# Heads of a latent-attention layer: output weights made in whole blocks, contexts ordered behind scores, query weights made at a border of the projection

## The chip, the cores and the metric

The kernel runs on one core of one Trainium2 chip. Time is device time in microseconds of one execution. Before the change three executions gave a median of 1743.06 us (1740.99 to 1744.13). One more execution was profiled.

## The reference, cut to what matters

Two layers over 4 sequences of 512 tokens and 1024 features. The part that the change touches is the attention of the second layer: 32 heads whose keys and values come from a latent of 64 numbers per token, shared by all heads.

```python
q = _rmsnorm(x @ wq_a.T, q_a_ln_w) @ wq_b.T            # 32 heads x (64 + 64 rotated)
kv = _rmsnorm(ckv, kv_a_ln_w) @ wkv_b.T                # from the latent, 64 wide
k_nope, v = (kv[..., :NOPE], kv[..., NOPE:])           # 64 and 128 per head
scores = jnp.einsum('bqhd,bkhd->bhqk', q_full, k_full) * softmax_scale
scores = jnp.where(causal[None, None], scores, jnp.finfo(scores.dtype).min)
attn = jax.nn.softmax(scores, axis=-1)
out = jnp.einsum('bhqk,bkhd->bqhd', attn, v).reshape(B, S, H * VD)
return out @ wo.T
```

Around it stand an attention over the batch, two feed-forward blocks with low-rank experts, layer norms and residual sums; the change leaves them alone.

## The kernel before

The kernel never forms keys or values per head. The key weights are multiplied into the query weights (`prepare_query`, L677), so that a query (`query`, L714) meets the latent itself; and the value weights are multiplied into the output weights (`prepare_output`, L1052), so that the attention's context stays 64 wide and two heads fill 128 rows.

Most products are in split precision: a float32 operand is kept as a high part in the fast format and a low part with the rest, and `matmul3` (L148) makes low x high, high x low, high x high (L150 to L152). "High" is a cast on ACT, "low" is a subtraction (operand minus high).

**Units.** The heads run as 128 units: 4 groups of 8 heads, in each the 4 sequences, in each the 8 heads. Unit u's steps are spread over the main loop (L1215): its query is made three units ahead and rotated (ACT copy L729, two DVE products into the one buffer `wA` L731 and L732, two POOL operations L733 and L734), split one unit ahead (DVE L741, POOL L742), its scores are made in four row tiles of 512, 384, 256 and 128 keys (`scores`, L898), each followed on DVE by mask and row minimum (L919) and on ACT by the exponential (L922); one unit later the probabilities are transposed on TensorE and copied out (`turn`, L934: two copies on ACT, one on DVE, L945). Three units later, for every second unit, `context` (L948) multiplies the probabilities of two heads with the latent: 16 float32 matmuls (L959) that each use 64 of the array's columns, two heads side by side, into one PSUM bank, and DVE divides by the sums (L962).

**Fillers.** Between these steps the loop advances a generator, `per` = three numbers of steps per unit (L1222), at three places: after the context, after the scores, after the next query. For a sequence after the first of a group the generator is the output projection of the sequence before it, `project` (L1008): for each pair of token tiles seven products of half matrices (names b11, t1, t2, b22, t3, b21, t4) in two steps of three matmuls each, into the PSUM banks `poa` and `pob` in turn, then DVE adds to the residual `xs` (L1036); ACT and POOL split the contexts (`cxh` L993, `cxl` L994), DVE forms their sums (`s`, L985). In the second half of a group's first sequence (in group 0: during all of it) the generator is `prepare_output`: it fills the 14 weight tiles of 128 x 512 (seven names, two of each) as high and low.

**How the output weights are made.** `block(n, half, at)` (L1063) multiplies one pair of heads' value weights with their output weights, 512 of 1024 columns at a time, into `poa` or `pob` (L1069, again 64 columns of the array and two side by side; the trace counts four matmuls per half). `kept` (L1077) copies a bank to one of six places in the buffer `raw` on ACT, `high` (L1080) casts on ACT, `low` (L1086) subtracts, `less` (L1094) takes differences. [...] After the second half of a pair `fetch_output` (L1043) loads the next pair into `slotC` by three DMAs; there is one such buffer. A block comes every two to four steps.

**Query weights.** `fetch_query` (L656) clears part of `raw` on POOL and issues six DMAs on SP; the main loop calls it twice in each group's last sequence, at units 0 and 4. `prepare_query` runs three units after the first (unit 3 of the last sequence) and four units after the second (unit 0 of the next group), in bank `pob`, between two fillers. `raw` has one buffer, for query weights and output weights in turn.

**What sets the order.** A planner orders the instructions of each engine at compile time: it walks through them by program order as priority and takes the first whose operands it expects to be ready by its own table of durations. Engines then run their list strictly in order, with semaphores. `tc.issue_after(ins)` adds an edge without a semaphore: what is traced inside it stands behind `ins` on that instruction's engine. All DMAs are issued on SP, also in order.

Of the kernel before, what the change touches and what calls it, by code (L numbers as in the profile page):

```python
# [46 lines left out]
def block_kernel(ctx: ExitStack, tc: tile.TileContext, a: dict, out: bass.AP):  # L47
# [100 lines left out]
    def matmul3(ps, ah, al, bh, bl, start, stop, **kw):  # L148

        T.matmul(ps, lhsT=al, rhs=bh, start=start, stop=False, **kw)  # L150
        T.matmul(ps, lhsT=ah, rhs=bl, start=False, stop=False, **kw)  # L151
        T.matmul(ps, lhsT=ah, rhs=bh, start=False, stop=stop, **kw)  # L152
# [693 lines left out]
    with ExitStack() as c2:  # L846
# [21 lines left out]
        scored = [None]  # L868
# [29 lines left out]
        def scores(u):  # L898
# [10 lines left out]
            for i in range(TPB - 1, -1, -1):  # L909
# [4 lines left out]
                else:  # L914
                    at = slice((i - 1) * P, i * P)
                    matmul3(ps[:, 0:n], h[:, at], l[:, at], kT[:, 0, 0:n], kT[:, 1, 0:n],
                            start=True, stop=True)
# [30 lines left out]
        def context(u):  # L948
# [7 lines left out]
            for j in range(TPB):  # L956
                w = S - j * P
                for n in range(2):
                    T.matmul(ps[n * KVR : (n + 1) * KVR, S - w : S], lhsT=k[:, j, :],  # L959
                             rhs=pTs[u + n][:, AT[j] : AT[j] + w], start=(j == 0),  # L960
                             stop=(j == TPB - 1))
# [46 lines left out]
        def project(g, b):  # L1008
# [7 lines left out]
            for j in range(0, TPB, 2):  # L1016
                at, xs, banks = {}, {}, {}
# [34 lines left out]
        def prepare_output(g, fetched):  # L1052
# [10 lines left out]
            def block(n, half, at):  # L1063
                nonlocal fetched
                wo, wv = fetched
                po[at] = pso.tile([P, 512], F32, name="po" + at)
                with ExitStack() if g else tc.issue_after(scored[0].ins):
                    for k in range(2):
                        T.matmul(po[at][k * KVR : (k + 1) * KVR, :], lhsT=wv[:, k, :],  # L1069
                                 rhs=wo[k][:, half * 512 : half * 512 + 512], start=True, stop=True)  # L1070
                if half and n + 1 < len(prs):
# [22 lines left out]
            def less(to, a0, a1):  # L1094
                if not {to, a0, a1} & set(po):
# [5 lines left out]
            def steps():  # L1101
                block(0, 0, "a")
                yield
                kept(0, "a")
                high("b11", "a")
                block(0, 1, "b")
                yield
                low("b11", "a")
                kept(1, "b")
                yield  # L1110
                less("b", "b", 0)
                block(1, 0, "a")
                yield
                high("t1", "b")
                kept(0, "b")
                kept(2, "a")
                high("b21", "a")
                yield
                low("t1", "b")
                low("b21", "a")  # L1120
# [610 lines left out]
```

## Time and profile before

| what | value |
|---|---|
| median of three executions | 1743.06 us |
| the profiled execution | 1745.28 us |
| its span, first to last instruction | 1743.1 us |
| TensorE busy (matmuls) | 1703.5 us, 98% |
| VectorE (DVE) busy | 1305.5 us, 75% |
| ScalarE (ACT) busy | 902.6 us, 52% |
| GpSimd (POOL) busy | 925.4 us, 53% |
| granted TensorE clock, mean | 0.998 |
| the heads, first to last unit | about 424 to 1490 us |
| from one context to the next in a steady stretch (802.56 to 818.66) | 16.1 us, two units |
| one block of output weights, half of the columns (L1069, four matmuls) | 1.08 us |
| one 128 x 512 subtraction on POOL (L1096) and on DVE (L1099), median | 1287 and 695 ns |

PE is TensorE, PEld its weight loads, SP the queue that issues DMAs. In a timeline a line gives start, duration, engine, line of the kernel, operation, written tile <- read tiles, shape, count, and in brackets the idle time before it with what ended it. In a line of waits stand the waiting group, what it waited for, the total, the number and the longest. In a window line stand the window, its length, and for PE, PEld, DVE, ACT and POOL the busy time with the number of instructions, then the clock, the DMA share and GB/s. Matmuls overlap in the pipeline, so the pitch from start to start is what counts, not a matmul's own duration; and a busy TensorE can still lose time between starts.

### The profile page before, as it was taken

The numbers are of one execution on the slowest core, as the hardware profiler recorded it, in microseconds if no ns is written. First come the engines' busy times: TensorE is split into PE (matmuls) and PEld (weight loads), VectorE is DVE, ScalarE is ACT, GpSimd is POOL, SyncE is SP. The second block draws the span as 40 slices with busy tenths as digits, with TensorE's granted clock in tenths as the row PEclk, the third lists the DMA queues.
The fourth block names the chain that finished last, engine by engine and source line by source line (L and its number), as shares of the span: only waits on it lengthen the run. The fifth ranks groups of instructions, "written<-read, shape, count | busy, mean of one in ns | idle before, by whom it ended". The sixth has DMA issues, their size and how long they took to land.

```text
span 1743.1 us, 31732 instructions
## 1 busy us (share of the span) xinstructions
PE 1703.5 (98%) x10536; PEld 1431.2 (82%) x10536; DVE 1305.5 (75%) x3494; ACT 902.6 (52%) x2316; POOL 925.4 (53%) x926
## 2 busy tenths in 40 slices
PE   7999999999999999999999999999999999999999
PEld 6899999998667877767787767777767777789998
DVE  7977885677877777787777777777778776687675
ACT  7422331366765555475555476555476555453332
POOL 0553541203666664666666656666566664575454
PEclk9999999999999999999999999999999999999999
DMA  4313543245324234353333353342454333853331
GB/s 195 134 40 118 181 164 114 89 139 164 115 87 150 81 109 150 104 176 114 110 122 113 105 201 97 105 140 95 133 168 151 103 111 120 303 196 122 138 117 62
DMA packets 131940, 228.17 MB, mean 131 GB/s; under 512 B 22272, under 2 KB 58752, under 8 KB 128448
## 3 DMA queue, kind: packets, MB, share of 16 engines
q1 hardware_dynamic: 131776, 226.13, 38.4%
q8 instruction: 84, 1.38, 0.3%
q14 instruction: 80, 0.66, 0.1%
HBM read 156.60 MB, written 71.83 MB: 131 GB/s over the span
## 4 chain that ended last, share of the span: by engine, by line
PE 85%; DVE 6%; DMA 3%; ACT 2%; issue 2%; POOL 2%; SPq 0%; ACTq 0%; DVEq 0%; POOLq 0%
PE psv L959 8%; PE pst L943 7%; PE po L150 4%; PE po L152 4%; PE po L151 4%; PE pss L150 4%; PE pss L151 4%; PE pss L152 3%; PE pob L150 3%; PE psq L150 3%; PE psq L151 3%; PE psq L152 3%; PE poa L150 3%; PE acc L150 3%; PE acc L152 3%; PE acc L151 3%
## 5 line engine op out<-in xcount | busy, mean ns | idle before, releaser
L922 ACT ACTIVATE p<-p,mn 128x512 f32<-128x512 f32 (+3 forms) x512 | 284.7, 558 | 218.0 <-DVE mn L919 217.6
L919 DVE CUSTOM_DVE_ANT_0 p<-pss,causal 128x512 f32<-128x512 f32 (+3 forms) x512 | 232.4, 486 | 27.4 <-PE pss L152 21.8
L733 POOL TENSOR_TENSOR qf<-qf,ropeT 64x512 f32<-64x512 f32 x128 | 164.6, 1286 | 166.4 <-ACT qf L729 163.4
L943 PE MATMUL pst<-ident,p 128*128 128x128 f32 x1280 | 186.4, 274 | 4.0 <-ACT pT L945 4.0
L734 POOL TENSOR_TENSOR qf<-qf,wA 64x512 f32<-64x512 f32 x128 | 164.4, 1285 | 29.9 <-DVE wA L732 23.4
L943 PEld LDWEIGHTS pst<-ident,p 128*128 128x128 f32 x1280 | 153.4, 141 | 31.4 <-ACT pT L945 8.7
L742 POOL TENSOR_TENSOR ql<-qf,qh 128x384 fp32r<-128x384 f32 x128 | 131.1, 1024 | 62.9 <-DVE qh L741 44.3
L994 POOL TENSOR_TENSOR cxl<-s,cxh 128x256 fp32r<-128x256 f32 x128 | 96.5, 762 | 120.6 <-ACT cxh L993 66.9
L945 ACT COPY pT<-pst 128x512 f32<-128x512 f32 x256 | 142.2, 577 | 23.2 <-PE pst L943 21.6
L150 PE MATMUL pss<-kT,ql 128*128 128x512 f32 (+2 forms) x384 | 142.8, 372 | 0.5 <-POOL ql L742 0.2
L150 PE MATMUL po<-w_h,hTl 128*128 128x384 f32 (+1 forms) x384 | 133.0, 346 | 0.5 <-DVE x L433 0.5
L151 PE MATMUL pss<-kT,qh 128*128 128x512 f32 (+2 forms) x384 | 130.9, 341 | 0.0
L152 PE MATMUL po<-w_h,hTh 128*128 128x384 f32 (+1 forms) x384 | 130.1, 339 | 0.0
L152 PE MATMUL pss<-kT,qh 128*128 128x512 f32 (+2 forms) x384 | 129.8, 338 | 0.0
L151 PE MATMUL po<-w_l,hTh 128*128 128x384 f32 (+1 forms) x384 | 129.7, 338 | 0.0
L945 DVE COPY pT<-pst 128x256 f32<-128x256 f32 x128 | 54.3, 424 | 94.2 <-PE pst L943 93.1
L729 ACT COPY qf<-psq 128x512 f32<-128x512 f32 x126 | 73.8, 586 | 71.9 <-PE psq L152 71.8
L731 DVE TENSOR_TENSOR wA<-psq,ropeT 32x512 f32<-32x512 f32 x126 | 87.7, 696 | 22.4 <-ACT qf L729 19.5
L994 POOL TENSOR_TENSOR cxl<-cx,cxh 128x256 fp32r<-128x256 f32 x96 | 73.5, 767 | 56.1 <-ACT cxh L993 53.5
L922 ACT ACTIVATION_READ_ACCUMULATOR p<-p,mn 128x1 f32 x512 | 97.0, 189 | 0.0
L150 PEld LDWEIGHTS pss<-kT,ql 128*128 128x128 f32 x384 | 72.1, 188 | 20.9 <-issue 3.6
L732 DVE TENSOR_TENSOR wA<-psq,ropeT 32x512 f32<-32x512 f32 x126 | 87.1, 691 | 1.7
(511 smaller groups left out, 4976.9 us busy)
## 6 DMA issues: line engine op xcount, KB each, us to landing
xs<-x_d SPq DMA_DIRECT2D x128, 256.0 KB
x_d<-xs SPq DMA_DIRECT2D x128, 256.0 KB
slotC<-in_woT_dram SPq DMA_DIRECT2D x32, 512.0 KB
rb<-r_d SPq DMA_DIRECT2D x128, 128.0 KB
w_t<-raw SPq DMA_DIRECT2D x32, 288.0 KB
x<-in_x_dram SPq DMA_DIRECT2D x16, 512.0 KB
x_d<-x SPq DMA_DIRECT2D x32, 256.0 KB
slotA<-q_d SPq DMA_DIRECT2D x8, 1024.0 KB
```

Source lines behind the costliest of these rows:

```text
L150: T.matmul(ps, lhsT=al, rhs=bh, start=start, stop=False, **kw)
L151: T.matmul(ps, lhsT=ah, rhs=bl, start=False, stop=False, **kw)
L152: T.matmul(ps, lhsT=ah, rhs=bh, start=False, stop=stop, **kw)
L733: G.tensor_tensor(f[mid], f[mid], ropeT[mid, 0, :], ALU.mult)
L734: G.tensor_tensor(f[mid], f[mid], t2[mid], ALU.add)
L742: G.tensor_tensor(l, f[:, P:S], f32(h), ALU.subtract)
L919: turn_of[0] = V.tensor_tensor_reduce(out=to, in0=ps[:, 0:n], in1=causal[:, S - n : S], scale=1.0, scalar=-NEG, op0=ALU.add, op1=ALU.min, ...
L922: A.activation(to, to, AF.Exp, bias=mn[:, i : i + 1], scale=-1.0, accum_out=rs[:, i : i + 1])
L943: T.transpose(ps[:, w : w + P], p[:, OF[i] + j * P : OF[i] + (j + 1) * P], ident)
L945: copy(pT[:, AT[js[0]] : AT[js[0]] + w], ps[:, 0:w])
L959: T.matmul(ps[n * KVR : (n + 1) * KVR, S - w : S], lhsT=k[:, j, :], rhs=pTs[u + n][:, AT[j] : AT[j] + w], start=(j == 0), stop=(j == TPB - 1))
L994: G.tensor_tensor(l, src, f32(h), ALU.subtract)
```

## The change

It has four parts.

1. `block(n)` makes both halves of a pair at once, into both banks, and then fetches the next pair. `steps` is written anew: the same twelve advances run twice (for blocks 0 and 1, then 2 and 3), with 24 advances in all. Intermediate differences go to `raw` and not back to PSUM, so that `low` runs on POOL for t1, b22, t2, t3 and t4 and on DVE for b11 and b21 only; `less` now always runs on DVE.
2. The steps per unit while output weights are made become 1, 1, 1 in group 0 (they were 0, 1, 2) and 2, 2, 2 later (they were 3, 2, 2 in two units of four).
3. The matmuls of a context are ordered behind the last matmul of the scores traced before them (`scored_`).
4. `prepare_query` moves from the main loop to the start of a pair in `project`, as soon as fetched weights are there, into the bank that the pair's first product does not use.

```diff
         T.matmul(ps, lhsT=ah, rhs=bl, start=False, stop=False, **kw)
-        T.matmul(ps, lhsT=ah, rhs=bh, start=False, stop=stop, **kw)
+        return T.matmul(ps, lhsT=ah, rhs=bh, start=False, stop=stop, **kw)
...
-                    matmul3(ps[:, 0:n], h[:, at], l[:, at], kT[:, 0, 0:n], kT[:, 1, 0:n],
-                            start=True, stop=True)
+                    scored_[0] = matmul3(ps[:, 0:n], h[:, at], l[:, at], kT[:, 0, 0:n],
+                                         kT[:, 1, 0:n], start=True, stop=True)
...
-            for j in range(TPB):
-                w = S - j * P
-                for n in range(2):
-                    T.matmul(ps[n * KVR : (n + 1) * KVR, S - w : S], lhsT=k[:, j, :],
-                             rhs=pTs[u + n][:, AT[j] : AT[j] + w], start=(j == 0),
-                             stop=(j == TPB - 1))
+            with tc.issue_after(scored_[0].ins):
+                for j in range(TPB):
+                    w = S - j * P
+                    for n in range(2):
+                        T.matmul(ps[n * KVR : (n + 1) * KVR, S - w : S], lhsT=k[:, j, :],
+                                 rhs=pTs[u + n][:, AT[j] : AT[j] + w], start=(j == 0),
+                                 stop=(j == TPB - 1))
...
             for j in range(0, TPB, 2):
+                if fetched_q:
+                    n, fetched = fetched_q.pop(0)
+                    wqs[n] = prepare_query(fetched, pso, "po" + "ab"[(1 + j // 2) % 2])
...
-            def block(n, half, at):
+            def block(n):
                 nonlocal fetched
                 wo, wv = fetched
-                po[at] = pso.tile([P, 512], F32, name="po" + at)
                 with ExitStack() if g else tc.issue_after(scored[0].ins):
-                    for k in range(2):
-                        T.matmul(po[at][k * KVR : (k + 1) * KVR, :], lhsT=wv[:, k, :],
-                                 rhs=wo[k][:, half * 512 : half * 512 + 512], start=True, stop=True)
-                if half and n + 1 < len(prs):
+                    for half, at in enumerate("ab"):
+                        po[at] = pso.tile([P, 512], F32, name="po" + at)
+                        for k in range(2):
+                            T.matmul(po[at][k * KVR : (k + 1) * KVR, :], lhsT=wv[:, k, :],
+                                     rhs=wo[k][:, half * 512 : half * 512 + 512], start=True, stop=True)
+                if n + 1 < len(prs):
                     fetched = fetch_output(g, prs[n + 1])
...
-                if not {to, a0, a1} & set(po):
+                if not {a0, a1} & set(po):
                     G.tensor_tensor(src(to), src(a0), src(a1), ALU.subtract)
...
             def steps():
-                block(0, 0, "a")
-                yield
-                kept(0, "a")
-                high("b11", "a")
-                block(0, 1, "b")
...
+                for n in (0, 2):
+                    block(n)
+                    if n:
+                        low("t4", 2)
+                    yield
+                    kept(1, "b")
+                    high("b11", "a")
+                    yield
+                    less(4, 1, "a")
+                    low("b11", "a")
+                    yield
+                    high("t1", 4)
+                    yield
+                    low("t1", 4)
+                    yield
+                    yield
+                    block(n + 1)
+                    yield
+                    kept(3, "b")
+                    high("b21", "a")
+                    less(5, "b", 4)
+                    yield
+                    high("b22", 3)
+                    low("b21", "a")
+                    less(2, "a", 5)
+                    less(0, "b", 1)
+                    yield
+                    high("t2", 5)
+                    low("b22", 3)
+                    yield
+                    high("t3", 0)
+                    low("t2", 5)
+                    yield
+                    high("t4", 2)
+                    low("t3", 0)
+                    if n:
+                        low("t4", 2)
+                    yield
...
-            per = ((4, 1, 0) if i % 2 else (1, 1, 0)) if b else (2 + (i < HG // 2 + 2), 2, 2) if i >= HG // 2 else (3, 3, 1)
+            per = ((4, 1, 0) if i % 2 else (1, 1, 0)) if b else (2, 2, 2) if i >= HG // 2 else (3, 3, 1)
             if B == 0:
-                per = (0, 1, 2)
+                per = (1, 1, 1)
...
-                if (b, i) == (NB - 1, 3) and g + 1 < NG:
-                    wqs[2 * g + 2] = prepare_query(wq_raw, pso, "pob")
-                if (b, i) == (0, 0) and g > 0:
-                    wqs[2 * g + 1] = prepare_query(wq_raw, pso, "pob")
...
                 if (b, i) in ((NB - 1, 0), (NB - 1, 4)) and g + 1 < NG:
-                    wq_raw = fetch_query(2 * g + 2 + i // 4)
+                    n = 2 * g + 2 + i // 4
+                    fetched_q.append((n, fetch_query(n)))
```

More of the change, by code (lines that the diff above doesn't have):

```diff
@@ L865, in block_kernel @@
         OF = {3: 0, 2: 512, 1: 896, 0: 1152}
-        scored = [None]
+        scored, scored_ = [None], [None]
         sums_of = [None]
@@ L1101, in steps @@
             def steps():
-                block(0, 0, "a")
-                yield
-                kept(0, "a")
-                high("b11", "a")
-                block(0, 1, "b")
[L1107 to L1117, printed above, removed]
@@ L1118, in steps @@
-                yield
-                low("t1", "b")
-                low("b21", "a")
-                block(1, 1, "b")
-                yield
-                high("b22", "b")
-                kept(3, "b")
-                yield
-                low("b22", 3)
-                less("b", "b", 0)
-                block(2, 0, "a")
-                yield
-                high("t2", "b")
-                kept(5, "a")
-                less(3, 3, 1)
-                yield
-                low("t2", "b")
@@ L1135, in steps @@
-                less("b", 2, "b")
-                high("b11", "a")
-                yield
-                high("t4", "b")
-                high("t3", 3)
-                low("b11", "a")
-                yield
-                low("t4", "b")
-                low("t3", 3)
-                block(2, 1, "a")
-                yield
-                kept(1, "a")
-                yield
-                less("a", "a", 5)
-                block(3, 0, "b")
-                yield
-                high("t1", "a")
@@ L1152, in steps @@
-                kept(5, "a")
-                kept(2, "b")
-                high("b21", "b")
-                yield
-                low("t1", "a")
-                low("b21", "b")
-                block(3, 1, "a")
-                yield
-                high("b22", "a")
-                kept(3, "a")
-                yield
-                low("b22", 3)
-                less("a", "a", 5)
-                yield
-                high("t2", "a")
-                less(3, 3, 1)
-                yield
@@ L1169, in steps @@
-                low("t2", "a")
-                less("a", 2, "a")
-                high("t3", 3)
-                yield
-                high("t4", "a")
-                low("t3", 3)
-                yield
-                low("t4", "a")
-                yield
+                for n in (0, 2):
[36 more added lines that the diff above has]
+                    yield
@@ L1213, in block_kernel @@
         filler = None
+        fetched_q = []
         cx = None
```

## The prediction

> **What bounds the kernel now.** First the page: shares of the engines, then the chain that ended last.
>
> ```profile
> PE 1703.5 (98%) x10536; PEld 1431.2 (82%) x10536; DVE 1305.5 (75%) x3494; ACT 902.6 (52%) x2316; POOL 925.4 (53%) x926
> ...
> PE 85%; DVE 6%; DMA 3%; ACT 2%; issue 2%; POOL 2%; SPq 0%; ACTq 0%; DVEq 0%; POOLq 0%
> ```
>
> TensorE is the bound. The change touches the heads alone (about 424 to 1490 us), so next I read TensorE's waits in 424 to 1486 us (total, times, longest), and the windows of the three stretches in which groups 1 to 3 make their output weights, with a steady stretch last.
>
> ```profile
> PE pst L943 <- ACT pT L945: 4.0, 5, 2.2
> PE psq L150 <- DVE wA L732: 1.0, 2, 0.8
> PE pob L150 <- POOL cxl L994: 0.9, 3, 0.3
> PE poa L1069 <- DMA slotC<-in_wv_dram: 0.5, 2, 0.3
> ...
> 736.90:767.40 30.50, 30.27 (x169) 18.90 (x168) 24.84 (x67) 24.33 (x62) 18.17 (x16) 1.00 0.62 203
> 1008.30:1038.40 30.10, 30.10 (x167) 18.80 (x166) 24.69 (x67) 24.32 (x62) 18.03 (x16) 1.00 0.60 206
> 1279.40:1309.80 30.40, 30.11 (x167) 18.83 (x166) 24.70 (x67) 24.33 (x62) 17.99 (x16) 1.00 0.60 204
> 802.60:834.80 32.20, 32.20 (x184) 25.31 (x186) 24.14 (x66) 18.08 (x51) 19.52 (x20) 1.00 0.41 138
> ```
>
> So plain waits in the heads come to under 7 us; the clock is granted in full. What else can be won is time inside the busy share. The timelines of TensorE show it: a block of output weights (L1069) alone among full-width matmuls, and then two that adjoin.
>
> ```profile
> 442.50 1.04 PE L943 MATMUL pst<-ident,p 128*128 128x128 f32 x8
> 443.47 1.08 PE L1069 MATMUL poa<-slotC 128*64 128x512 f32 x4
> 444.48 0.50 PE L150 MATMUL psq<-slotA,wql 128*128 128x512 f32 x1
> 444.81 0.40 PE L151 MATMUL psq<-slotA,wqh 128*128 128x512 f32 x1
> 445.05 0.39 PE L152 MATMUL psq<-slotA,wqh 128*128 128x512 f32 x1
> ...
> 739.52 0.60 PE L1069 MATMUL poa<-slotC 128*64 128x512 f32 x2
> 739.95 1.03 PE L1069 MATMUL pob<-slotC 128*64 128x512 f32 x4
> ```
>
> Eight transposes at 0.11 end at 443.38; the lone block starts 0.09 later. Its two side-by-side pairs need 0.84 (adjoining ones stand 0.43 apart), but the next start is at +1.01: 0.17 more. The matmul after that follows at 0.33, not 0.23 to 0.24 as the next does: 0.10. Together 0.36, of which a block inside a run still pays some 0.05: I price one separate run of half-width (128*64) matmuls at 0.30 us.
>
> Last, the longest wait, at 490 us, on ACT and on PE:
>
> ```profile
> 487.13 0.62 ACT L1083 CAST t31h<-raw 128x512 fp32r<-128x512 f32 x1 [2.48 <-POOL raw L1096]
> 487.65 0.72 ACT L922 ACTIVATE p<-p,mn 128x512 f32<-128x512 f32 x1
> ...
> 487.82 0.39 PE L150 MATMUL pss<-kT,ql 128*128 128x512 f32 x1
> 490.46 0.44 PE L943 MATMUL pst<-ident,p 128*128 128x128 f32 x2 [2.25 <-ACT pT L945]
> ```
>
> ACT stands 2.48 us before one cast, waiting for POOL's subtraction (`less(3,3,1)`, L1096); queued behind it are the exponentials and pT copies, and TensorE waits for those.
>
> **The change, part by part.**
>
> *Fewer separate runs.* The trace has 88 runs of L959 and L1069 matmuls in the heads. Contexts need 64. The other 24: 17 lone half blocks (5 in group 0, 4 in each later group), 4 contexts of which two matmuls start ahead of the next scores (493.73, 763.08, 1034.19, 1305.60), and 3 split by a query at the groups' borders (691.30, 962.66, 1233.75). After it, group 0 advances three steps per unit, so its blocks, six steps apart, come straight after a context each: none alone. Groups 1 to 3 advance six steps per unit: every second block has no context beside it, 2 each, 6 in all. The edge behind the scores forbids the 4 early pieces; it doesn't forbid the 3 border splits, since these already stand behind their scores. 24 falls to 9: 15 x 0.30 = 4.5 us saved. In steady units the context stands behind the 384-wide scores already, so the edge moves nothing there. Bounds: 1.5 us (all 16 blocks alone) to 7.2 us (none). [...]
>
> *Subtractions leave POOL, low halves go to it.* Counted per group from the steps: ACT copies 24 to 18 (kept 10 to 4, high 14), DVE 16 to 12, POOL 6 to 10. `less` is all on DVE, so no cast waits for POOL any more. That takes the 2.25 us at 490 and three waits of 0.49 us at 776, 1047 and 1319 (the same cast of t31, 0.97 us late at 774.85): 2.25 + 1.47 = 3.7 us. What ACT waits for next is DVE, whose `less` now comes a step earlier than its `high`; DVE is 81% busy there (24.84 of 30.50), and one such wait is in the trace (t21h behind L1099, 1.51 us, with no wait of TensorE beside it). Bounds: 0 to 5 us, the upper one with the context that stretched from 493.73 to 495.31 behind it.
> The work itself I cost at nothing. 6 copies less x 0.59 and 4 DVE subtractions less x 0.69 are freed beside TensorE's work. POOL gains 4 x 1.29 = 5.2 us per group; its cover is the 12.3 us that it is idle in each 30.5 us stretch. If that cover is gone, all 4 x 5.2 = 21 us could show; that is the second rival.
> [...]
>
> *Both halves at once.* The 16 block matmuls per group stay. A block now needs both banks and holds slotC for 2 x 0.84 us; the next load is issued after it, as before after the second half. Before, the end of a block at 740.9 to the next at 747.01 took 6.1 us, with a wait of 0.23 for the load. Three loads per group now stand between blocks one unit (30.5 / 4 = 7.6 us) apart. There were two waits for loads, 0.5 us in all; if six of the nine intervals now wait 0.25 each, that is 1.0 us more. Nothing else queues on SP: the same four fetches are issued per group, `slotC` free at the same point. Bounds: -0.5 (no wait) to +10.8 us (the third rival).
>
> *Query weights at a border of the projection.* `prepare_query` keeps its 8 short matmuls (0.9 us), 2 ACT copies, 1 POOL and 1 DVE subtraction. The first of a group is made two steps earlier, in the same unit; the second one unit earlier (unit 7 of the last batch instead of unit 0 of the next). It takes the bank that the pair's first product doesn't use, so its eviction lies beside six 0.23 us matmuls before the second product wants the bank. `raw` comes free earlier; the fetch with its POOL memset (0.31 us) and six DMAs is issued where it was, three units ahead (over 20 us), and the first fetch was taken up at 491.94 for a use at 633. POOL and DVE at that place are 62% and 75% busy in the steady window. Zero; bounds -0.9 (the three border splits, which follow the second preparation by 1.5 us, vanish) to +2 (each of six evictions 0.3 us late).
>
> **Sum:** -4.5 - 3.7 + 1.0 + 0 = -7.2 us. The profiled execution took 1745.28 us (span 1743.1), 2.2 above the median of 1743.06; I take the difference off the median: 1735.9 us.
>
> **The rivals.**
> 1. *It wins more.* Setting each TensorE start against its pitch in an undisturbed place (0.23 us for 512 columns, 0.18 for 384, 0.12 for 256, 0.11 for a transpose, 0.43 for a side-by-side pair) leaves 9.5 of the 63.6 us from 436 to 500, 5.7 of the 49.2 from 736.8 to 786, and only 5.2 of the steady 140.6 from 1329 to 1470. Above the steady rate that is 7.1 us in group 0 and 3.9 in each later group: 18.8. If all of it goes but the six blocks alone (1.8): 17.0, 1726.1 us. For it: three ways of waiting go at once. Against: I can name only 8.2 of it.
> 2. *POOL becomes late, slower than before.* Over a stretch POOL has 4 units x 3.6 (L733, L734, L742) + 10 x 1.29 + 2 x 0.74 = 28.8 us of work in 28 to 30 us, if all low halves are done inside it. DVE's wA has one buffer, which POOL's L734 frees; a rotation queued behind one low half per unit holds DVE, then the scores. 12 units x 1.29 = 15.5 us, less the 7.2: 1751.4. It decides once POOL is more than two units behind, since queries run three units ahead. For it: POOL ran without a gap from 481.7 to 487.1 when two such operations met two rotations. Against: no one waits for low halves until the projection a unit later, and three of six before were done after the stretch.
> 3. *It is given back by the loads, no change.* If blocks come as early as their place in the program, then between the first and second of a pair lie 0.35 + 0.22 + 1.09 + 1.38 (rest of a unit: scores, transposes, query) and 0.69 + 0.53 (next scores) = 4.3 us, where 6.1 are needed; the other intervals have a context more (2.4) and suffice. 2 x 1.8 x 3 groups = 10.8 us lost against 8.2 gained: 1745.7. Against: the order before held the next block back to 0.25 us of its load.
>
> **How the numbers follow.** Mine 0.54, the first rival 0.12, the second 0.14, the third 0.20, a tenth of that beyond +0.2%. Faster by over 0.2% is mine and the first: 0.66; same 0.18; slower 0.16. The range goes up to the third's 1746 and down halfway from my own low end to the first's 1726: 1729.5. My own case alone: 1733 (4.5 + waits at 5 + 0.5 of loads) to 1739 (runs at 1.5 us). A measurement of this kernel tells about 0.2% (3.5 us) from no change.
>
> **What would show it.** Right: about 73 runs of half-width matmuls; no ACT cast behind L1096 or its successor; no TensorE wait over 1 us near 490; group period (271.1 us between 965.18 and 1236.28) shorter by 1.5 to 2; the steady context period still 16.1 us. Wrong: waits of TensorE on slotC over 1 us, DVE wA behind POOL, or a longer steady period because the planner, which orders the whole, chose otherwise in places that I took as fixed.

## The result: slower by 0.4%

The changed kernel takes 1749.23 us (median of six executions, 1748.17 to 1751.76), the one before took 1742.44 us beside it (six, 1740.88 to 1744.55). The ratio is 1.0039, with a 95% interval of 1.0029 to 1.005. The profiled spans are 1747.7 and 1743.1 us. I had predicted 1735.9 and a gain.

The page of the changed kernel, shares of the engines and the chain that ended last:

```profile
PE 1700.1 (97%) x10536; PEld 1429.0 (82%) x10536; DVE 1297.8 (74%) x3478; ACT 896.1 (51%) x2292; POOL 947.3 (54%) x942
...
PE 86%; DVE 5%; POOL 3%; ACT 2%; issue 1%; DMA 1%; SPq 0%; POOLq 0%; DVEq 0%; ACTq 0%
```

The counts moved as predicted: 24 copies fewer on ACT, 16 operations fewer on DVE, 16 more on POOL, in a kernel of four groups. Nothing on this page shows a loss; POOL is busy 54% instead of 53%. The waits of TensorE in the heads (424 to 1495 us; total, times, longest) do:

```profile
PE pss L150 <- POOL ql L742: 5.7, 3, 2.8
PE pob L150 <- DVE xs L1040: 3.3, 3, 1.3
PE pst L943 <- ACT pT L945: 2.3, 4, 0.7
PE psq L150 <- ACT pT L945: 1.3, 6, 0.2
```

The wait of 2.25 us at 490 is gone. In its place the scores wait twice, 2.8 us each, for POOL's low half of the queries (`ql`, which L742 writes), and the projection waits 0.7 to 1.3 us in each later group for DVE's residual sums (L1040).

Where the time went can be counted from context to context. The table gives, from the starts of the first context matmul of every second unit, the time from the first to the sixth context (group 0's output weights lie there), and the three group periods after it, each from the sixth context of a group to the sixth of the next, for this and all later runs. These spans are of the one profiled execution of each kernel; the medians are of all its executions. Runs are stretches of half-width matmuls (contexts and blocks) without another matmul between them.

| kernel | median us | ratio to before, 95% | first to sixth context | groups 1, 2, 3 | runs |
|---|---|---|---|---|---|
| before | 1742.4 to 1742.8 | 1 | 75.5 | 271.3, 271.1, 271.4 | 88 |
| the change | 1749.23 | 1.0029 to 1.0050 | 80.9 | 271.6, 272.1, 271.9 | 79 |
| e1: parts 1 and 2 | 1750.35 | 1.0035 to 1.0062 | 80.3 | 271.4, 272.1, 271.2 | 86 |
| e2: part 3 | 1742.38 | 0.9992 to 1.0009 | 74.5 | 271.2, 271.4, 271.2 | 84 |
| e3: part 4 | 1738.75 | 0.9973 to 0.9990 | 75.5 | 269.8, 269.9, 270.1 | 85 |
| e4: the change, POOL's order mended | 1740.18 | 0.9985 to 1.0002 | 72.4 | 270.9, 271.3, 271.7 | 79 |
| e5: the change, group 0's low halves on DVE | 1744.10 | 0.9998 to 1.0015 | 74.4 | 271.2, 272.2, 272.0 | 81 |
| e6: before, all differences on DVE | 1742.43 | 0.9989 to 1.0007 | 74.9 | 270.8, 271.6, 271.1 | 90 |
| e7: parts 3 and 4 | 1738.96 | 0.9972 to 0.9989 | 74.7 | 269.9, 270.4, 270.3 | 81 |
| e8: part 4, differences on DVE | 1738.52 | 0.9967 to 0.9986 | 74.9 | 270.5, 270.0, 270.0 | 87 |
| e9: e4 without part 3 | 1740.09 | 0.9975 to 0.9993 | 73.4 | 270.7, 270.7, 270.5 | 83 |
| e10: e4, old pace in groups 1 to 3 | 1743.10 | 0.9990 to 1.0007 | 72.4 | 271.6, 272.1, 272.0 | 73 |
| e11: parts 3 and 4, differences on DVE | 1741.18 | 0.9980 to 0.9998 | 75.5 | 271.5, 270.9, 270.9 | 82 |

So the change loses 5.4 us in group 0 and 0.3, 1.0 and 0.5 in the later groups. Those small numbers are the sum of a larger loss and a gain, which the experiments below take apart.

What happens at the first of the two stalls is in POOL's timeline of the changed kernel:

```profile
459.67 1.29 POOL L733 TENSOR_TENSOR qf<-qf,ropeT 64x512 f32<-64x512 f32 x1 [1.21 <-ACT qf L729]
461.03 1.28 POOL L1094 TENSOR_TENSOR t20l<-raw,t20h 128x512 fp32r<-128x512 f32 x1
462.27 1.40 POOL L1094 TENSOR_TENSOR t40l<-raw,t40h 128x512 fp32r<-128x512 f32 x1
463.63 1.28 POOL L1094 TENSOR_TENSOR t30l<-raw,t30h 128x512 fp32r<-128x512 f32 x1
464.99 1.26 POOL L734 TENSOR_TENSOR qf<-qf,wA 64x512 f32<-64x512 f32 x1
466.33 2.12 POOL L742 TENSOR_TENSOR ql<-qf,qh 128x384 fp32r<-128x384 f32 x2
```

and in TensorE's, over the same time:

```profile
464.35 0.38 PE L943 MATMUL pst<-ident,p 128*128 128x128 f32 x2
467.55 0.80 PE L150 MATMUL pss<-kT,ql 128*128 128x512 f32 x1 [2.83 <-POOL ql L742]
468.15 0.63 PE L151 MATMUL pss<-kT,qh 128*128 128x512 f32 x1
468.57 0.63 PE L152 MATMUL pss<-kT,qh 128*128 128x512 f32 x1
```

Three low halves of output weights stand in POOL's list between the two halves of one rotation, L733 and L734, and the low half of a query that is wanted at once stands behind that. DVE's product `wA`, for which L734 needs to wait, ended at 461.03 in the trace, and `qh` (L741) at 462.53. Without the three, by an estimate from these durations, L734 would have ended near 462.3 and `ql` near 463.6, before TensorE ran out at 464.73. The weight `t30l`, made at 463.63, is first read at 524.0: work that had 60 us was put ahead of work that had about one. The same three stand there again at 494.44 to 498.32 (t21l, t41l, t31l), with the second wait of 2.72 us at 500.96. In the order before, over the same stretch (459 to 500 us), no more than two operations of the output weights stood ahead of a query's.

The last two lines of TensorE show a second loss. Matmuls of 512 columns follow each other at 0.42 us, not at 0.23: the granted clock is 0.50 after the stall. The windows behind the stalls of the changed kernel (bounds, length, busy time with counts for PE, PEld, DVE, ACT, POOL, then the granted clock, DMA share, GB/s), those of before behind its wait of 2.25 us, and those of e1 (described below) behind the first of its two waits of 2.6 us:

```profile
467.50:470.90 3.40, 3.35 (x8) 2.11 (x10) 1.37 (x5) 1.22 (x4) 2.23 (x2) 0.50 0.00 0
470.90:474.00 3.10, 3.10 (x18) 1.36 (x16) 1.28 (x2) 0.61 (x2) 1.26 (x1) 0.59 0.00 0
500.90:504.30 3.40, 3.34 (x9) 2.11 (x10) 1.61 (x4) 0.81 (x2) 2.49 (x4) 0.52 0.59 168
```

```profile
490.40:493.70 3.30, 3.24 (x15) 2.75 (x15) 3.10 (x8) 2.34 (x6) 3.00 (x3) 0.67 0.18 50
493.70:497.00 3.30, 3.30 (x13) 1.81 (x13) 1.11 (x7) 2.23 (x6) 1.42 (x2) 0.81 0.51 162
```

```profile
469.70:473.00 3.30, 3.26 (x11) 1.99 (x13) 2.19 (x5) 0.81 (x2) 2.23 (x2) 0.69 0.00 0
473.00:477.00 4.00, 4.00 (x20) 1.95 (x17) 1.16 (x3) 1.37 (x4) 1.27 (x1) 0.83 0.00 0
```

Each window's length times what its clock lacks of 1 is my estimate of the time lost to the clock: 0.50 x 3.4 + 0.41 x 3.1 + 0.48 x 3.4 = 4.6 us for the change, 0.33 x 3.3 + 0.19 x 3.3 = 1.7 us for before. With the waits, 2.8 + 2.7 + 4.6 = 10.1 against 2.25 + 1.7 = 4.0. That is 6.1 us, about the 5.4 by which group 0 is longer. The estimate holds to some 2 us only: for e1 it gives 5.2 + 1.7 against 4.0, so 2.9, and its group 0 is 4.8 longer than before. The part of the clock also differs from one execution to the next: over the six of the change the mean granted clock was 0.995 to 0.999, the longest (1751.76 us) had 0.995, and two with 0.999 still took 1748.17 and 1748.63.

### The profile page after: what moved, and what is told of

The parts are those of the page before. It is cut to its first block, busy times and chain, and to the rows that moved or that the text cites. A ratio compares the mean times of both kernels' runs of the same rounds, so it can differ in the third digit from the quotient of the medians.

```text
span 1747.7 us, 31685 instructions
## 1 busy us (share of the span) xinstructions
PE 1700.1 (97%) x10536; PEld 1429.0 (82%) x10536; DVE 1297.8 (74%) x3478; ACT 896.1 (51%) x2292; POOL 947.3 (54%) x942
## 4 chain that ended last, share of the span: by engine, by line
PE 86%; DVE 5%; POOL 3%; ACT 2%; issue 1%; DMA 1%; SPq 0%; POOLq 0%; DVEq 0%; ACTq 0%
PE psv L960 8%; PE pst L943 7%; PE po L150 4%; PE po L152 4%; PE po L151 4%; PE pss L150 4%; PE pss L151 3%; PE pss L152 3%; PE pob L150 3%; PE poa L150 3%; PE psq L150 3%; PE psq L151 3%; PE psq L152 3%; PE acc L150 3%; PE acc L152 3%; PE acc L151 3%
## 5 line engine op out<-in xcount | busy, mean ns | idle before, releaser
L733 POOL TENSOR_TENSOR qf<-qf,ropeT 64x512 f32<-64x512 f32 x128 | 164.5, 1285 | 163.4 <-ACT qf L729 159.8
L734 POOL TENSOR_TENSOR qf<-qf,wA 64x512 f32<-64x512 f32 x128 | 164.6, 1286 | 27.2 <-DVE wA L732 20.6
L742 POOL TENSOR_TENSOR ql<-qf,qh 128x384 fp32r<-128x384 f32 x128 | 131.8, 1031 | 66.1 <-DVE qh L741 27.8
```

The source lines that it names most:

```text
L733: G.tensor_tensor(f[mid], f[mid], ropeT[mid, 0, :], ALU.mult)
L734: G.tensor_tensor(f[mid], f[mid], t2[mid], ALU.add)
L742: G.tensor_tensor(l, f[:, P:S], f32(h), ALU.subtract)
```

## The experiments

**e1 to e3: each part alone.** Parts 1 and 2 belong together (the new `steps` with the new pace); part 3 is the edge, part 4 the query weights.

e1, before with whole blocks, new steps, differences on DVE and the new pace:

```diff
-            def block(n, half, at):
+            def block(n):
...
-                if not {to, a0, a1} & set(po):
+                if not {a0, a1} & set(po):
...
+                for n in (0, 2):
...
-            per = ((4, 1, 0) if i % 2 else (1, 1, 0)) if b else (2 + (i < HG // 2 + 2), 2, 2) if i >= HG // 2 else (3, 3, 1)
+            per = ((4, 1, 0) if i % 2 else (1, 1, 0)) if b else (2, 2, 2) if i >= HG // 2 else (3, 3, 1)
...
-                per = (0, 1, 2)
+                per = (1, 1, 1)
```

> The kernel before with the block, step and per-unit parts of the change alone (no edge behind scores, query weights made where they were). In the profile of the changed kernel TensorE waits twice in group 0 for POOL's ql, 2.83 us at 467.55 and 2.72 us at 500.96; both times POOL runs three low halves (t2, t4, t3) between the two operations of one rotation, and after each wait the granted clock is 0.50 to 0.59 for some 5 us. Theory A (POOL's order): these two places cost about 9 us with the slow clock, and this part alone makes them: 4 to 7 us slower than before, with both waits of 2 us or more on ql in group 0. Theory B (the loss comes from the edge or from the border): this part alone is within 2 us of before or faster, without the two waits.

e2, before with the contexts' edge:

```diff
+                    scored_[0] = matmul3(ps[:, 0:n], h[:, at], l[:, at], kT[:, 0, 0:n],
...
+            with tc.issue_after(scored_[0].ins):
+                for j in range(TPB):
...
```

> The kernel before with the edge alone: contexts ordered behind the scores traced before them. Theory A: no slower than before; the four contexts of which two matmuls started ahead become whole, so 84 separate runs of half-width matmuls for 88, 1 us faster, 0 to 2. Theory B: slower than before by 2 us or more, with a TensorE wait in the heads that the kernel before lacks.

e3, before with the query weights made in the projection:

```diff
+                if fetched_q:
+                    n, fetched = fetched_q.pop(0)
+                    wqs[n] = prepare_query(fetched, pso, "po" + "ab"[(1 + j // 2) % 2])
...
-                if (b, i) == (NB - 1, 3) and g + 1 < NG:
-                    wqs[2 * g + 2] = prepare_query(wq_raw, pso, "pob")
-                if (b, i) == (0, 0) and g > 0:
-                    wqs[2 * g + 1] = prepare_query(wq_raw, pso, "pob")
...
-                    wq_raw = fetch_query(2 * g + 2 + i // 4)
+                    n = 2 * g + 2 + i // 4
+                    fetched_q.append((n, fetch_query(n)))
```

> The kernel before with the query weights' part alone: made at the start of a pair in the projection. Theory A: within 1.5 us of before; the three splits of contexts at the groups' borders go (0.9 us), the group period stays 271 us within 0.5. Theory B: slower by 2 us or more, the period of groups 1 to 3 longer by 0.7 us or more each.

Measured: e1 1750.35 us, with TensorE's two waits on `ql`, 2.6 us each, at 469.7 and 502.7. That is 7.7 us over the kernel before, a little more than the 4 to 7 expected: parts 1 and 2 alone lose as much as the whole change, without the edge and without part 4. e2 changes nothing that can be told (1742.38). Its first to sixth context is 1 us shorter, and the runs fall from 88 to 84 since the four early pieces are gone, yet the group periods stay. A new wait took the place of what was saved, by TensorE's waits of e2:

```profile
PE poa L150 <- DVE t41l L1093: 4.5, 3, 1.5
PE pst L943 <- ACT pT L945: 2.5, 2, 2.3
```

e3 gains 3.9 us (ratio 0.9973 to 0.999) where I had counted zero, and neither of its expectations holds: each group is 1.3 to 1.5 us shorter. The lines of TensorE at a group's border, before:

```profile
688.65 0.40 PE L150 MATMUL pss<-kT,ql 128*128 128x512 f32 x1
689.05 0.44 PE L943 MATMUL pst<-ident,p 128*128 128x128 f32 x2
689.24 0.48 PE L151 MATMUL pss<-kT,qh 128*128 128x512 f32 x1
689.55 0.40 PE L152 MATMUL pss<-kT,qh 128*128 128x512 f32 x1
689.79 1.05 PE L688 MATMUL pob<-raw 128*128 128x128 f32 x8
...
691.30 2.15 PE L959 MATMUL psv<-pT,slotA 128*64 128x512 f32 x10
693.38 0.50 PE L150 MATMUL psq<-slotA,wql 128*128 128x512 f32 x1
...
694.96 0.86 PE L959 MATMUL psv<-pT,slotA 128*64 128x256 f32 x6
```

and in e3 at the same context:

```profile
691.90 0.38 PE L943 MATMUL pst<-ident,p 128*128 128x128 f32 x2
692.04 0.48 PE L150 MATMUL pss<-kT,ql 128*128 128x512 f32 x1
692.35 0.39 PE L151 MATMUL pss<-kT,qh 128*128 128x512 f32 x1
692.58 0.39 PE L152 MATMUL pss<-kT,qh 128*128 128x512 f32 x1
...
693.44 2.37 PE L959 MATMUL psv<-pT,slotA 128*64 128x512 f32 x16
695.74 0.50 PE L150 MATMUL poa<-b110h,cxl 128*128 128x512 f32 x1
```

Before, the eight short matmuls of the query weights push the scores and the context apart: transposes stand between two matmuls of one product, and the context is in two pieces with a query between. From the context ahead of the first query weights to the end of the border, with both query weights in it, before takes 17.0 + 16.1 + 16.1 + 14.2 + 24.8 = 88.2 us, e3 17.0 + 16.1 + 17.0 + 16.1 + 20.7 = 86.9. TensorE has no wait there that the profile counts in either kernel, so the 1.3 us lie between starts: I had seen the split context (0.3 per group) and not the pieces of scores. I did not set the remaining 1 us against single places.

Added up, the three give 7.7 - 0.2 - 3.9 = 3.6 us over before, the change itself 6.8. Together they cost more than alone. Where, can be read from the same starts of contexts. The border is counted from the thirteenth context of a group to the second of the next, the output weights from the second to the sixth context of groups 1 to 3; each number is the sum of three groups. What lies between, from the sixth to the thirteenth, is 338.5 to 338.9 us in all kernels.

| kernel | group 0, first to sixth context | borders | output weights, groups 1 to 3 |
|---|---|---|---|
| before | 75.5 | 264.8 | 210.5 |
| the change | 80.9 | 261.4 | 215.7 |
| e1: parts 1 and 2 | 80.3 | 264.9 | 211.2 |
| e2: part 3 | 74.5 | 264.9 | 210.3 |
| e3: part 4 | 75.5 | 261.0 | 210.2 |
| e4: the change, POOL's order mended | 72.4 | 261.4 | 213.7 |
| e7: parts 3 and 4 | 74.7 | 261.2 | 211.0 |
| e9: e4 without part 3 | 73.4 | 261.1 | 212.0 |
| e10: e4, old pace in groups 1 to 3 | 72.4 | 261.1 | 215.8 |

The change has the gain of part 4 at the borders, 3.4 us. It gives back more than that in the later groups' output weights, 5.2 us, of which no part alone shows more than about 0.7. TensorE's waits there, of 0.15 us and more, come to 6.17 us against 2.87 before and 3.25 in e1: on ACT's copies of probabilities (0.68 per group) and on DVE's sums (0.73, 1.28, 1.27), where e1 waits for POOL's `cxl` (1.01, 1.01, 0.82). The rest lies between starts, and I did not set it against places. Which two parts meet there is in part open: with POOL's order mended, taking the edge away shortens these stretches by 1.7 us (e4 and e9), and no run takes the edge or part 4 alone out of the change.

**e4 and e5: order or amount.** Both keep the change whole but for POOL's low halves. e4 leaves the work on POOL and gives each low half two edges without semaphores, behind the last rotation and the last split that were traced:

```diff
+    rotated = [None, None]
...
-        G.tensor_tensor(f[mid], f[mid], t2[mid], ALU.add)
+        rotated[0] = G.tensor_tensor(f[mid], f[mid], t2[mid], ALU.add)
...
-        G.tensor_tensor(l, f[:, P:S], f32(h), ALU.subtract)
+        rotated[1] = G.tensor_tensor(l, f[:, P:S], f32(h), ALU.subtract)
...
-                    G.tensor_tensor(l, src(at), f32(h), ALU.subtract)
+                    with tc.issue_after(rotated[0].ins), tc.issue_after(rotated[1].ins):
+                        G.tensor_tensor(l, src(at), f32(h), ALU.subtract)
```

> The changed kernel with one edge more: each low half that POOL makes for the output weights stands behind the last rotation's second operation and the last split of a query traced before it. POOL's work is the same, only its order differs: no longer three low halves inside one rotation. Theory A (order): the two waits of 2.8 us on ql go and with them the slow clock: 7 to 10 us faster than the changed kernel, so 1739 to 1742.5, a little faster than before. Theory C (amount: POOL has too much to do in group 0 wherever it stands): the low halves now delay the next split instead, TensorE still waits 2 us or more for ql in group 0, and the time stays above 1746.

e5 takes the low halves of group 0 away from POOL:

```diff
-                if at not in po:
+                if g and at not in po:
```

> The changed kernel, but in group 0 the low halves of the output weights are subtracted on DVE instead of POOL (ten of 1.28 us leave POOL, ten of about 0.69 us go to DVE). Theory A (the last two rotations before the stalls stand behind three low halves in POOL's list): TensorE's two waits for the low half of the queries near 464.7 and 498.2 us (2.8 us each) go, and with them the slow clock behind them; the first to the sixth context takes 72 to 76 us instead of 80.9, and the time is 1740 to 1743 us. Rival (the lost time belongs to the new sequence of steps and DVE is late next): TensorE waits for DVE instead, on wA, on the masks or on a low half, group 0 stays above 78 us, 1746 to 1750 us.

Measured: e4 1740.18 us, 9 us less than the change (8 by the two ratios to before) with the same operations on the same engines. POOL's timeline of e4 at the place of the first stall (lines after L711 are numbered one or two higher):

```profile
461.55 1.28 POOL L734 TENSOR_TENSOR qf<-qf,ropeT 64x512 f32<-64x512 f32 x1 [3.52 <-ACT qf L730]
463.06 1.27 POOL L735 TENSOR_TENSOR qf<-qf,wA 64x512 f32<-64x512 f32 x1 [0.23 <-DVE wA L733]
464.69 1.00 POOL L743 TENSOR_TENSOR ql<-qf,qh 128x384 fp32r<-128x384 f32 x1 [0.36 <-DVE qh L742]
465.65 1.29 POOL L1096 TENSOR_TENSOR b220l<-raw,b220h 128x512 fp32r<-128x512 f32 x1
466.89 1.42 POOL L1096 TENSOR_TENSOR t20l<-raw,t20h 128x512 fp32r<-128x512 f32 x1
```

The rotation is whole, the query's low half follows at once, the output weights come behind. TensorE has no wait on `ql` of 0.3 us or more in the heads, and the first to the sixth context takes 72.4 us, 8.5 less than in the change and 3.1 less than before it. So the order of the list made the loss of group 0 and not the amount of work on POOL. Of the 5.2 us in the later groups' output weights e4 takes back 2.0. e5 answers the rest for group 0: without those operations on POOL the waits on `ql` are gone too, but for one of 0.2, and group 0 takes 74.4 us; smaller ones on DVE stand there instead (0.55 on masks at 464.9, 0.74 on a copy of probabilities at 499.9, 1.29 on the sums at 510.6), and the time is 1744.1, just above what I had put for it. In group 0 the work is better on POOL, in a better order, than on DVE: 72.4 against 74.4 us.

Half the duration on DVE (0.69 us for a subtraction of 128 x 512, against 1.29 on POOL) did not decide: in group 0 e4, with the low halves on POOL, is 2.0 us ahead of e5. The medians are 3.9 us apart, but e4 mends POOL's order in the later groups too, which e5 leaves as in the change, so they don't compare the engines alone.

**e6 and e8: the wait of 2.25 us by itself.** e6 is before with one piece of part 1, every difference on DVE; e8 adds part 4.

```diff
-                if not {to, a0, a1} & set(po):
-                    G.tensor_tensor(src(to), src(a0), src(a1), ALU.subtract)
-                    return
```

> The kernel before with one line of the change alone: every difference of the output weights (less) is formed on DVE, none on POOL. Theory A (my second term, re-sized): the wait of the cast of t31 for POOL goes, so TensorE's 2.25 us near 490 and the slow clock behind it, and three waits of 0.49 near 776, 1047 and 1319. The term said 3.7 us; with the slow clock it should be 5 to 6: 1736.5 to 1739 us, first to sixth context 71 to 73 us instead of 75.5. Rival (a wait takes the place of the one removed): the difference on DVE is queued behind masks and the cast waits for DVE as long as for POOL; 1741 to 1744 us with a wait of over 1.5 us left near 490.

> The kernel before with part 4 (query weights at a border of the projection, -3.9 us alone) and with every difference of the output weights on DVE. If the two are apart, as their places are (677 to 740 against 476 to 500 and 770 to 790 in each group), the gains add: with 3 to 6 us for the second, 1733 to 1736 us and faster than both kernels. If the wait of the cast comes back on DVE: 1738 to 1740 us.

Measured: e6 1742.43 us, no difference (0.9989 to 1.0007). The wait at 490 is gone, and TensorE's waits in the heads of e6 are short; three of the lines:

```profile
PE pss L150 <- POOL ql L742: 0.9, 3, 0.4
PE psq L150 <- DVE wA L732: 0.8, 1, 0.8
PE pss L150 <- DVE mn L919: 0.7, 1, 0.7
```

Yet the first to the sixth context is only 0.6 us shorter. Of the 4.0 us that the wait and its slow clock took, 1.4 came back as other waits there (0.7 on masks at 464.7, 0.3 and 0.4 on `ql` at 467.2 and 496.6), and 0.6 as two more separate runs (11 and not 9 of blocks and pieces of contexts between 440 and 500 us). That leaves 1.4 unexplained (4.0 - 1.4 - 0.6, less the 0.6 that was gained). Both of my theories for e6 fail in part: the wait did go, and the time did not. e8, 1738.52, is e3's time, in line with e6 being worth nothing; my sum of 1733 to 1736 for it is wrong for the same reason. That it lies in the range that I had put for a wait on DVE is no support for that case: the cast's wait did not come back.

**e7 and e11: combinations without the whole blocks.** e7 is e2 and e3 together, e11 e7 with the line of e6.

> The kernel before with parts 3 and 4 together: contexts behind scores, query weights at a border of the projection. Theory A (the parts add): 0 and -3.9 us, so 1738 to 1740 us; the 1.5 us wait on DVE for t41l that the edge alone brought in at 775, 1047 and 1318 stays. Rival (the two meet at the groups' borders, since both settle where the contexts there stand): the contexts that the planner split at 763, 1034 and 1305 are whole, the wait on DVE is gone or halved, and the time falls to 1733 to 1736 us.

> The kernel before with parts 3 and 4 and every difference on DVE, without the whole blocks. Parts 3 and 4 gave 1739.0, part 4 with the differences on DVE 1738.5. Theory A (TensorE is filled, and what one takes away from its waits near 490 and 775 comes back as other waits and as contexts in pieces): 1737.5 to 1739.5 us. Rival (the edge keeps the contexts whole and lets the removed wait of 2.25 us show): 72 to 73 us from the first context to the sixth, 1734 to 1737 us.

Measured: e7 1738.96, as the sum of the two, with the wait on `t41l` of 1.5 us still in each group. e11 1741.18 us, worse than e7 and a miss of both ranges: the wait of 2.25 us is gone, with twelve waits of up to 0.8 us on DVE's masks in its place (4.9 us in all) and a load that is 1.3 us late.

**e9 and e10: what the whole blocks are worth once POOL is mended.** e9 is e4 without the edge of part 3. e10 is e4 with the pace of before in groups 1 to 3:

```diff
-            per = ((4, 1, 0) if i % 2 else (1, 1, 0)) if b else (2, 2, 2) if i >= HG // 2 else (3, 3, 1)
+            per = ((4, 1, 0) if i % 2 else (1, 1, 0)) if b else (2 + (i < HG // 2 + 2) if g else 2, 2, 2) if i >= HG // 2 else (3, 3, 1)
```

> The changed kernel with POOL's low halves held behind the last rotation and the last split (as in the run that held them so, 1740.2 us), and without part 3, the contexts' edge behind the scores. It asks what the whole blocks are worth once POOL's order is mended. Theory A (the edge is what keeps the runs of half-width matmuls few, and is worth 1 us in group 0 and nothing later): 81 to 87 runs, 1740 to 1743 us. Rival (the edge holds contexts too long and makes the waits on the contexts' low halves, 0.8 to 1.0 us in each group): those waits fall under 0.4 us, 1736 to 1739 us.

> The changed kernel with POOL's low halves held as before, and in groups 1 to 3 the older pace of steps (3, 2, 2 in two units of four instead of 2, 2, 2), so that the output weights are done some 4 us earlier. Theory A (the waits of 0.8 to 1.0 us near 779, 1050 and 1322 on the contexts' low halves come from low halves of the output weights that run late on POOL): they fall under 0.4 us and a group takes 270 to 270.5 us instead of 270.9 to 271.7; 1737 to 1739 us. Rival (blocks fall out of step with the contexts, and stand alone more often): 82 runs or more, 1740 to 1742 us.

Measured: e9 1740.09 us with 83 runs, e4's time. The edge is worth 1.0 us in group 0, as I had put it, but not nothing later: without it the three periods are 2.0 us shorter together. The waits near 779, 1050 and 1320 are 1.55, 1.53 and 1.09 us without the edge, 0.89, 0.98 and 1.33 with it: two longer and one shorter, none under 0.4 as the rival asked. e10 has 73 runs, the number that I had predicted for the change (I had put six blocks alone and three contexts split; here each context is whole, and three blocks of each later group stand alone). And it takes 1743.1 us, by the medians 2.9 more than e4 with its 79, outside the ranges of both theories. The intervals of the two ratios to before overlap; the three group periods, 1.7 us longer together, point the same way. TensorE's waits of e10 show what stands against the runs saved:

```profile
PE pss L150 <- DVE mn L920: 5.4, 10, 0.8
PE pob L150 <- DVE xs L1041: 2.9, 2, 1.5
PE psq L150 <- DVE wA L733: 2.5, 5, 0.8
PE pob L150 <- POOL cxl L996: 1.8, 3, 0.8
```

Six runs fewer are 1.8 us; the waits on the masks alone are 4.5 us more than e4's 0.9. My theory for e10 (low halves of the output weights run late, and earlier ones would free the contexts' splits) fails: the waits near 780 and 1052 grew from 0.89 and 0.98 us to 1.45 and 1.46, and they end on DVE's sums now; only the one near 1324 fell, from 1.33 to 0.77. The rival fails as well, since there are fewer runs and not more.

The fastest are e3, e7 and e8, 1738.5 to 1739.0: part 4, with or without the edge, and without the whole blocks. They beat the kernel before by 0.2% and the change by 0.6%. No median with whole blocks came below 1740.

## Why the prediction was wrong

**The step that failed** is "The work itself I cost at nothing ... POOL gains 4 x 1.29 = 5.2 us per group; its cover is the 12.3 us that it is idle in each 30.5 us stretch." The cover was an average over a stretch of four units, read in groups 1 to 3. In group 0 the new steps issue three low halves in neighbouring steps, the planner put them between two dependent operations of one rotation, and nothing of the idle time around it was of use: 3 x 1.3 us stood ahead of an operation that could have started at once. In its place the runs show two stalls of TensorE on `ql`, 2.83 and 2.72 us, with an estimated 4.6 us of slow clock behind them: group 0 took 80.9 us instead of 75.5, and 72.4 when e4 put the same operations behind the rotations. The amount was covered, as e4 shows; the place was not. What I should have looked for is what else stands in POOL's list when three low halves come in one unit, and how soon TensorE wants what is behind them.

**The second rival** had the direction and the mechanism ("a rotation queued behind one low half"), and I gave it 0.14 with the wrong place and condition. It put the loss into groups 1 to 3, through DVE's buffer `wA`, and to be decided "once POOL is more than two units behind". POOL was behind by less than one unit, `wA` held nothing up, and what waited was the scores, directly for `ql`. Three units of lead for the queries did not help, since the split is made one unit ahead. Two pile-ups of three were enough, 5.6 us of waits and 4.6 of slow clock, where I had asked for twelve at 1.29. That its 1751.4 us lies near the measured 1749.2 is luck.

**Runs of half-width matmuls.** I said 73; the change has 79. Group 0 went as predicted, all its blocks beside contexts. In groups 1 to 3 three blocks of four stand alone, not two, and two contexts of each group (755.48 and 773.12 in the first of them) are cut in pieces of ten and six. The price of 0.30 us for one separate run stands: from the last start ahead of a half-width run to the second start behind it, TensorE is 0.34 or 0.35 us behind the pitches of the undisturbed matmuls in 60 of 77 cases of the kernel before and in 55 of 63 of the change (runs next to a wait, or with transposes behind them, left out), of which a block inside a run still pays some 0.05. But the term "15 x 0.30 = 4.5 us saved" was wrong in kind: e10 has just 15 fewer and is no faster than e4, which has nine fewer. Fewer runs did not save time there: in e10 longer waits, most of them on DVE (5.4 us on the masks, where e4 has 0.9), stood in their place.

**The wait on POOL's difference.** 3.7 us predicted; e6, which removes just this, measures 0 (at most 1.9 us by its interval). The wait itself was worth more than I took, 2.25 us and 1.7 of slow clock, and still its removal brought nothing that can be told. "What ACT waits for next is DVE" was the right question; the bound "0 to 5" held, and I took the wrong end of it.

**Loads.** +1.0 predicted over the 0.5 us of before; the changed kernel has one wait of 0.2 us on `slotC` in the heads. The third rival is out.

**Query weights.** Zero with bounds of -0.9 and +2; measured -3.9. The mechanism behind the lower bound, no context split at the border, was right; the pieces of scores and transposes around the preparation were missing from it. I also took the second preparation for one unit earlier, as in the program. In TensorE's list it moved by 27 us, over three units of 8, from 689.79 to 662.62: away from the border, to right behind a whole context.

**What was to show it.** No TensorE wait over 1 us near 490: so, but one of 2.72 stands at 501. No cast behind the successor of L1096: almost, ACT waits 1.7 us in three for L1104 before `t21h`. The steady context period of 16.1 us: unchanged. A group period shorter by 1.5 to 2: it is longer by 0.3 to 1.0. A steady stretch disturbed by the planner: no.

**The accounts.** The predicted sum was -4.5 - 3.7 + 1.0 + 0 = -7.2; measured is +6.8. By the runs alone it is: whole blocks with their steps and pace +7.7, the edge -0.2, the query weights -3.9, and 3.2 us that the parts cost together beyond their sum. By the places in the trace of the change it is: group 0 +5.4, made by POOL's order as e4 shows; the borders -3.4; the output weights of groups 1 to 3 +5.2, for which my sum had a gain, and whose cause is shown only in part. A reading to put right: POOL is 61% busy in the steady window (19.52 of 32.20 us), not 62%; nothing hangs on it.

## What to carry to other kernels

Idle time of an engine covers added work only if the work can be put into it. Where a planner orders the engines' lists by estimates, ask of each moved operation what it can stand in front of, and when that is due; an edge that holds work with 60 us of slack behind work that is due now was worth 8 to 9 us here, 8.5 of them in the one stretch with the stalls. A wait or a late start seen on the busiest engine need not be worth its length: in e6, 4.0 us of wait and slow clock gave 0.6. Take it away alone on the chip before it goes into a sum. And a period that hardly changes can hide a gain and a loss: cut it at the places that the change touches.

## What the runs showed of the hardware

**A stall of TensorE cost more than its length where the clock fell behind it.** In the traces of the two kernels the granted clock falls from 1.00 to 0.50: before, for 3.41 us at 51.20 and at 491.52; in the change, for 6.83 us at 466.63, for 3.41 us at 500.76 and in the last us of the span. From the end of one slow spell to the start of the next lie 436.91 us before (54.61 to 491.52) and 27.30 us in the change (473.46 to 500.76), 128 and 8 times 3.41. Windows of this length, laid from the slow spells, show what went ahead of them. First the kernel before at its wait of 2.25 us, then e1 at its two waits of 2.6 us; a window's length less the busy time of PE, its first number behind the comma, is TensorE's idle time:

```profile
488.11:491.52 3.41, 1.16 (x7) 0.97 (x7) 1.40 (x6) 3.41 (x12) 2.27 (x3) 1.00 0.38 152
491.52:494.93 3.41, 3.41 (x13) 2.07 (x11) 2.44 (x6) 2.31 (x5) 3.17 (x4) 0.50 0.38 114
```

```profile
467.55:470.96 3.41, 1.22 (x6) 1.04 (x6) 0.83 (x5) 0.96 (x3) 3.33 (x4) 1.00 0.00 0
470.96:474.37 3.41, 3.41 (x14) 1.66 (x13) 2.43 (x6) 1.52 (x4) 2.31 (x2) 0.50 0.00 0
498.27:501.68 3.41, 1.76 (x10) 1.36 (x10) 1.79 (x8) 2.82 (x10) 3.25 (x4) 1.00 0.02 6
501.68:505.10 3.42, 2.44 (x13) 1.71 (x15) 1.40 (x4) 0.71 (x3) 3.34 (x4) 1.00 0.43 135
```

The first wait of e1 leaves 2.19 us idle in one window, and the next is slow. The second, just as long, is divided between two windows (1.65 and 0.98 us idle), and the clock stays at 1.00. The windows ahead of the slow spells of the two kernels had 2.25 us idle (before, 488.11), 1.91 (before, 47.79), 1.90 (the change, 463.22), 2.51 (the change, 497.35) and 2.38 (the change, 1743.21). The length of one wait alone does not tell: near 51 us TensorE waits 1.72 us in the kernel before, with 1.91 us idle in the window, and 1.71 us in the change, with 1.30 us idle; the first was followed by a slow spell, the second was not. By estimate, from 0.50 over 3.41 us, a slow window that TensorE fills costs at most 1.7 us. Why the first stall of the change brought two of them, the second behind a slow window with 0.92 us idle, is open.

Behind each of the four waits of about 2.25 us near 490 (before, e2, e3 and e7) the clock was lower: 0.67, 0.54, 0.64 and 0.50 over the next 3.2 to 3.3 us. Behind waits of 1.5 to 1.55 us it was 1.00: from 774.5 to 782 us in e7, from 779 to 782 and from 1049.7 to 1053 in e9.

**Query weights between other work.** Eight matmuls (1.05 us together, at 689.79 in the kernel before), put where scores and a context meet, cost about 1.3 us per group more than behind a whole context, without a wait in the profile. Only a comparison from context to context showed it; what makes up the larger part of it is not shown.
